# Layer 0's unit order and one set of adjacency transposes for layers 1 and 2 in a four-layer graph network

## The chip, the cores and the metric

The kernel runs on one core of one Trainium2 chip. The time is device microseconds of one execution; the profile shows one execution with the busy time of each engine: TensorE (PE, with its weight loads as PEld), VectorE (DVE), ScalarE (ACT), GpSimd (POOL) and SyncE (SP, which only issues transfers). Before the change the kernel takes 2264.58 us, the median of three runs between 2263.07 and 2265.11.

## What is computed

128 graphs of 64 nodes with 256 features pass through four layers; after each, the layer's input is added and each node's row is normalised (mean and variance over its 256 features).

- Layer 0 works on the first 25 nodes. For each of five fixed groups of them it applies two graph convolutions (256 to 512 to 256 features) with the group's adjacency plus identity, scaled on both sides by 1/sqrt(degree), and adds the results with softmax weights. The other 39 nodes only pass the norm.
- Layer 1 is one such convolution over all 64 nodes: `out = D (A + I) D x W + b`, D the diagonal of 1/sqrt(degree).
- Layer 2 is a polynomial in the row-normalised adjacency P = A / rowsum: `out = (w0 + w1 P + w2 P^2 + w3 P^3) h W + b`, with a leaky ReLU.
- Layer 3 is five steps of a gated recurrent unit (GRU): messages `h W_l` are summed along nonzero edges and drive the gates r, z and n. Each step needs the one before.

All arithmetic is fp32.

## The kernel before, in words

**Chunks.** After layer 0 the graphs go in 16 chunks of eight. A chunk is held as four pairs of graphs, so that one 128x128 block-diagonal matrix holds the adjacencies of two graphs. Two chunks at a time run through layer 3, and their steps alternate row by row, so that one chunk's gates (DVE, ACT, POOL) lie under the other's matrix products (PE).

**Order.** The instruction order on PE is written out by hand: PE runs what the program text says, in that order. On the other engines a planner orders the instructions by the order of the text and by when it thinks an operand is ready. Every engine runs its own queue strictly in order, so an instruction that waits holds up all behind it.

**Layer 0** runs over 16 units, each one group of nodes for up to four tiles of graphs (groups 1, 2, 3, 4, then 0; the last seven units are group 0). For a unit:

- `load0` brings the adjacency rows `a` and the features `xg`. For the first three units POOL issues the `xg` loads, for all others SyncE does.
- `prep` (L336) adds the identity, sums the degrees (L354), takes their power on POOL (`inv_sqrt`, L122), forms the block-diagonal A0 on DVE (L359) with the constant mask `block0`, transposes it on PE (L367) and scales it into AT on DVE (L370).
- `aggregate` (L380) multiplies the features by AT, `hidden` (L394) and `support` (L408) apply the two weight matrices, `add` (L430) aggregates again and adds into F. For group 0 `finish` (L465) transposes back, adds the input and takes the norm.

A loop over i (L525) staggers these: add(i-1), aggregate(i+1), support(i), finish(i-1), hidden(i+1), prep(i+2), and then one tile of the other 39 nodes (`load_others`, `others`, `store_others`: load xo, statistics at L133, scale at L148, store). All of these loads and stores are issued by SyncE, and all weights of the five groups are requested at the start (L502 to L506).

**Layers 1 and 2** of a chunk are the generator `mid` (L210), with a `yield` between the steps: Ab (block-diagonal adjacency), A01 (its nonzero pattern), the degree factors; A1, both factors of layer 1 applied before and after its transpose; Ab divided by the row sums; two sets of four transposes (L241 for layer 1, L247 for layer 2); the polynomial by two sets of products (L255, L261), with `gather` (L201, aggregation for layer 1) between them; the products with layer 1's weights (L270) and the norm; the second gather; the products with layer 2's weights (L286) and the norm. `layernorm` (L127) does statistics on DVE, the power on POOL (L138) and the scaling on ACT (L145) in one go.

For chunks 0 and 1 these steps are placed within the last layer-0 units (`early`, L518). For later chunks they are the `filler` of the layer-3 rows: one step at the end of every row, and one in the middle of every even row (L823).

**Layer 3.** A row s of the loop at L804 issues, for one chunk x and the chunk w of the row before, the seven products of a two-by-two block scheme for the gates r and z (`x.rz(i)`) and n (`x.n(i)`, `w.n(i)`). `Gates.product` (L663) accumulates in a PSUM bank and copies partial sums away on ACT (L671). `w.n(3)` and `w.n(4)` end in the update of h; `w.turn` transposes it (L695), `w.close` gathers the next messages.

PSUM is two pools: five banks (`pg`) and three (`pt`). Layer 0 takes from both in turn, the steps of `mid` and the transposes of layer 3 from the three.

Of the kernel before, what the change touches and what calls it, by code (L numbers as in the profile page):

```python
# [1 line left out]

# [1 line left out]

# [5 lines left out]
F32 = mybir.dt.float32  # L10
AF = mybir.ActivationFunctionType
# [56 lines left out]
def gnn_stack(  # L68
# [55 lines left out]
        nc.vector.scalar_tensor_tensor(o, v, 0.0, r, op0=ALU.not_equal, op1=ALU.mult)  # L124
        return o

    def layernorm(y, by="v", n=NP, r=128):  # L127

        by = (by * n)[:n]
        st = small.tile([128, NP, 6], F32, name="st")  # L130
        mv = small.tile([128, NP, 2], F32, name="mv")
        for p in range(n):
            nc.vector.bn_stats(st[:r, p, :], y[:r, p, :])  # L133
            nc.vector.bn_aggr(mv[:r, p, :], st[:r, p, :])
        ve = small.tile([128, NP], F32, name="ve")
        nc.vector.tensor_scalar(ve[:r, :n], mv[:r, :n, 1], EPS_LN, None, op0=ALU.add)  # L136
        rs = small.tile([128, NP], F32, name="rs")
        nc.gpsimd.tensor_tensor(rs[:r, :n], ve[:r, :n], mhalf[:r, :n], ALU.pow)  # L138
        if "a" in by:
            nb = small.tile([128, NP], F32, name="nb")  # L140
            nc.vector.scalar_tensor_tensor(nb[:r, :n], mv[:r, :n, 0], -1.0, rs[:r, :n], op0=ALU.mult, op1=ALU.mult)  # L141
        for p in range(n):
            v = y[:r, p, :]
            if by[p] == "a":
                nc.scalar.activation(v, v, AF.Identity, bias=nb[:r, p : p + 1], scale=rs[:r, p : p + 1])  # L145
            else:
                e = nc.vector if by[p] == "v" else nc.gpsimd
                e.tensor_scalar(v, v, mv[:r, p, 0:1], rs[:r, p : p + 1], op0=ALU.subtract, op1=ALU.mult)  # L148

    def interleave(*gens):  # L150
        gens = list(gens)
# [58 lines left out]
    def mid(c):  # L210

        a64 = adjs.pop(c)


        Ab = keep.tile([128, NP, 128], F32, name="Ab", bufs=1)
        nc.vector.tensor_mul(
            Ab.rearrange("p q (b m) -> p q b m", b=2),
            a64[:, :, None, :].to_broadcast([128, NP, 2, N]),
            pair[:, None, :, :].to_broadcast([128, NP, 2, N]),
        )  # L220
        A01 = keep.tile([128, NP, 128], F32, name="A01", bufs=4)
        nc.vector.tensor_scalar(A01, Ab, 0.0, None, op0=ALU.not_equal)
        rsum = small.tile([128, NP], F32, name="rsum")
        nc.vector.tensor_reduce(rsum, a64, AX.X, ALU.add)
        rdeg = small.tile([128, NP], F32, name="rdeg")
        nc.vector.tensor_scalar(rdeg, rsum, 1.0, None, op0=ALU.add)
        rinv = small.tile([128, NP], F32, name="rinv")
        nc.vector.tensor_scalar(rinv, rsum, 1e-9, None, op0=ALU.add)
        nc.vector.reciprocal(rinv, rinv)
        dinv1 = inv_sqrt(rdeg, NP, 128, "d1")  # L230
        A1 = keep.tile([128, NP, 128], F32, name="A1", bufs=1)
        nc.vector.tensor_add(A1, Ab, ident[:, None, :].to_broadcast([128, NP, 128]))
        nc.vector.tensor_mul(A1, A1, dinv1[:, :, None].to_broadcast([128, NP, 128]))
        nc.vector.tensor_mul(Ab, Ab, rinv[:, :, None].to_broadcast([128, NP, 128]))
        yield


        AT1 = keep.tile([128, NP, 128], F32, name="AT1", bufs=1)
        p = psum("pT1").rearrange("p (q n) -> p q n", q=NP)
        for q in range(NP):  # L240
            nc.tensor.transpose(p[:, q, :], A1[:, q, :], ident)  # L241
        nc.vector.tensor_mul(AT1, p, dinv1[:, :, None].to_broadcast([128, NP, 128]))

        poly = keep.tile([128, NP, 128], F32, tag="poly", name="poly3", bufs=2)
        p = psum("pT2").rearrange("p (q n) -> p q n", q=NP)
        for q in range(NP):
            nc.tensor.transpose(p[:, q, :], Ab[:, q, :], ident)  # L247
        nc.vector.scalar_tensor_tensor(
            poly, p, cw[:, 3:4], cI[:, 2, None, :].to_broadcast([128, NP, 128]), op0=ALU.mult, op1=ALU.add
        )  # L250
        yield
        xt = xts.pop(c)
        p = psum("pp").rearrange("p (q n) -> p q n", q=NP)
        for q in range(NP):
            nc.tensor.matmul(p[:, q, :], Ab[:, q, :], poly[:, q, :], start=True, stop=True)  # L255
        poly = keep.tile([128, NP, 128], F32, tag="poly", name="poly1", bufs=2)
        nc.vector.tensor_add(poly, p, cI[:, 1, None, :].to_broadcast([128, NP, 128]))
        ag = gather(xt, AT1, "ag1")
        p = psum("pp").rearrange("p (q n) -> p q n", q=NP)
        for q in range(NP):  # L260
            nc.tensor.matmul(p[:, q, :], Ab[:, q, :], poly[:, q, :], start=True, stop=True)  # L261
        poly = keep.tile([128, NP, 128], F32, tag="poly", name="poly0", bufs=2)
        nc.vector.tensor_add(poly, p, cI[:, 0, None, :].to_broadcast([128, NP, 128]))
        yield
        for u in range(NP // 2):
            p = psum("pd").rearrange("p (q d) -> p q d", q=2)
            for h in range(2):
                q = 2 * u + h
                for k in range(2):
                    nc.tensor.matmul(  # L270
                        p[:, h, :], ag[:, k, q * 128 : (q + 1) * 128], L1W[:, k, :], start=k == 0, stop=k == 1
                    )
            nc.vector.tensor_add(xt[:, 2 * u : 2 * u + 2, :], p, xt[:, 2 * u : 2 * u + 2, :])
        nc.vector.tensor_add(xt, xt, l1bs[:, None, :].to_broadcast([128, NP, D]))
        layernorm(xt, "a")
        yield


        ag = gather(xt, poly, "ag2")
        yield  # L280
        for u in range(NP // 2):
            p = psum("pd").rearrange("p (q d) -> p q d", q=2)
            for h in range(2):
                q = 2 * u + h
                for k in range(2):
                    nc.tensor.matmul(  # L286
                        p[:, h, :], ag[:, k, q * 128 : (q + 1) * 128], L2W[:, k, :], start=k == 0, stop=k == 1
                    )
            v = keep.tile([128, 2, D], F32, name="v", bufs=1)
            nc.scalar.activation(v, p, AF.Identity, bias=cb)  # L290
            nc.vector.scalar_tensor_tensor(v, v, 0.2, v, op0=ALU.mult, op1=ALU.max)
            nc.vector.tensor_add(xt[:, 2 * u : 2 * u + 2, :], v, xt[:, 2 * u : 2 * u + 2, :])
        layernorm(xt, "a")
        state[c] = (xt, A01)
        yield

# [11 lines left out]
    with ExitStack() as c0:  # L308
# [6 lines left out]

        loads, A, AG, HG, S2, Z, XO = {}, {}, {}, {}, {}, {}, {}

        def load0(i):
            u = UNITS[i]

            qa = [nc.scalar, nc.sync] if i == 0 else [nc.sync]
# [3 lines left out]
            for t, (b0, nb) in enumerate(u.tiles):  # L325
                b = slice(b0, b0 + nb)
                row = 0
                for f, m in RUNS[u.g]:
# [1 line left out]
                    row += nb * m  # L330
                    w = u.n if u.g < 2 else NE
                    qa[t % len(qa)].dma_start(a[rows, t, :w], adj[b, f : f + m, 0:w])
                    qx.dma_start(xg[rows, t, :], x[b, f : f + m, :])
            loads[i] = a, xg

        def prep(i):  # L336
# [162 lines left out]
        b1 = const(b1T, [128, NG * 4], "b1", nc.scalar, w0)  # L499
        b2c = const(b2.rearrange("g (k p) -> p (g k)", p=128), [128, NG * 2], "b2", nc.scalar, w0)  # L500
        fw = spread(fusion_w, NG, "fw", w0, nc.scalar)
        for g in (1, 2, 3, 4, 0):  # L502
            nc.sync.dma_start(W1[:, g], w1[g].rearrange("(k p) e -> p k e", p=128))
            nc.sync.dma_start(W2[:, g], w2[g].rearrange("(k p) e -> p k e", p=128))
            if g in (1, 2):
                load0(g)  # L506

        def products(l, q):

# [7 lines left out]

        early = both(mid(0), mid(1))  # L518

        def stage(f, i, first=0):  # L520
            if first <= i < NU:
                f(i)

        g0 = next(i for i, u in enumerate(UNITS) if u.g == 0)
        for i in range(-2, NU + 1):  # L525
# [1 line left out]
                stage(load0, i + 3)  # L527
            stage(add, i - 1)
            stage(aggregate, i + 1)
            if i > g0 + 2:  # L530
                next(early, None)
            stage(support, i)
            if i == NU:
                folds = [products(0, q) for q in range(3)]
            stage(finish, i - 1, g0)
            if i > g0:
                next(early, None)
            stage(hidden, i + 1)
            if i > g0:
                next(early, None)  # L540
            stage(prep, i + 2)
            for f, o in ((store_others, i - 1), (others, i), (load_others, i + 2)):
                if 0 <= o < 10:
                    f(o)
# [15 lines left out]
            elif i == 1:  # L560
# [9 lines left out]
                    mask = const_later(maskT, [128, B // 2], "mask")  # L570
                brz = wp.tile([128, 4], F32, name="brz")
                nc.vector.tensor_add(brz, bih[:, 0:4], bhh[:, 0:4])


                cI = wp.tile([128, 3, 128], F32, name="cI")
                for k in range(3):
                    nc.vector.tensor_scalar(cI[:, k, :], ident, cw[:, k : k + 1], None, op0=ALU.mult)
            elif i == 4:

                ih = keep.tile([128, 4, 2, D], F32, tag="RZ", name="ih", bufs=2)  # L580
# [59 lines left out]
    class Gates:  # L640
# [22 lines left out]
        def product(self, i):  # L663
# [3 lines left out]
            if i in (1, 6, 7, 4):  # L667
                self.multiply(self.a, i)
                if i != 4:
                    c = self.copies[i] = work.tile([128, 2, H], F32, tag="copy", name=f"c{i}", bufs=4)  # L670
                    nc.scalar.copy(c, self.a)  # L671
                if i == 7:
                    nc.vector.tensor_add(C[:, :, 1, H:], self.d, self.copies.pop(7))  # L673
            elif i == 2:
# [129 lines left out]
    for s in range(NCH * L):  # L804
# [15 lines left out]
        if w:  # L820
            w.n(3)
        x.rz(6)
        if t % 2 == 0:  # L823
            next(filler, None)
        x.rz(5)
        x.rz(7)
        x.n(1)
# [91 lines left out]
```

## Time and profile before

| | us |
|---|---|
| time, median of 3 | 2264.58 |
| span of the profiled execution | 2265.5 |
| PE busy / idle in it | 2198.4 / 67.1 |
| DVE, ACT, POOL busy | 1328.4, 1047.5, 587.5 |
| PE busy in 0 to 123 us (layer 0, first seven units) | 92.9 |
| PE busy in 123 to 223 us (layer 0, next units) | 100.0 |
| PE busy in 223 to 385 us (layer 0's end, chunks 0 and 1, weights of layer 3) | 148.9 |
| PE busy in 411 to 600 us, 600 to 838 us (layer 3) | 188.4 of 189, 236.6 of 238 |
| PE busy in 2220 to 2265.5 us (tail) | 29.8 |

A line of the profile names the source line, the engine, the operation, the output and the inputs, the shapes and a count, then the busy time and the mean of one, and last the idle time of the engine just before, with what ended it. In a list of single instructions the first number is the start in us and the second the length. A matrix product in fp32 appears as two records (L241 and the other transposes as one). In the list of waits each line says which engine at which line waited for which, how long in total, how often, and the longest.

### The profile page before, as it was taken

The page shows a single profiled execution, that of the slowest core. Times are in us where ns is not written, and L with a number is a line of the kernel's source. Part 1 is how long each engine was busy: PE and PEld are TensorE (multiplying, and loading weights), DVE is VectorE, ACT ScalarE, POOL GpSimd, SP SyncE. Part 2 cuts the span into 40 slices and gives each one's busy share as a digit, 9 for nine tenths or more (in the row PEclk, how much of TensorE's full clock was granted, in tenths as well). Part 3 has the DMA queues.
Part 4 walks back from the last instruction along what each step waited for, and adds up shares of the span by engine and source line. Part 5 has one row for each costly group of instructions (what it writes and reads, how often), then busy time and mean ns, then how long its engine had stood idle before and what let it go on. Part 6 is the DMA issues. An engine that isn't in the chain of part 4 may idle for free.

```text
span 2265.5 us, 30226 instructions
## 1 busy us (share of the span) xinstructions
PE 2198.4 (97%) x11590; PEld 1920.0 (85%) x11590; DVE 1328.4 (59%) x2927; ACT 1047.5 (46%) x1930; POOL 587.5 (26%) x639
## 2 busy tenths in 40 slices
PE   5999999999999999999999999999999999999997
PEld 4777778888888888888888888988889888888886
DVE  4433446655765656556666575566665665556546
ACT  2333334454545454544544544445454545455453
POOL 3210104222232222322322222222222222223222
PEclk9999999999999999999999999999999999999998
DMA  7530200000000001000100010000000000000000
GB/s 203 167 104 12 64 21 28 3 1 3 19 22 1 3 10 31 1 3 1 38 3 3 1 38 3 3 1 24 17 1 1 19 10 1 1 6 15 1 1 19
DMA packets 53892, 51.12 MB, mean 23 GB/s; under 512 B 20598, under 2 KB 48630, under 8 KB 53748
## 3 DMA queue, kind: packets, MB, share of 16 engines
q1 hardware_dynamic: 49524, 43.90, 6.4%
q0 software_dynamic: 1936, 4.83, 0.8%
q8 instruction: 91, 1.49, 0.3%
q10 hardware_dynamic: 2288, 0.47, 0.1%
q14 instruction: 53, 0.43, 0.1%
HBM read 32.40 MB, written 16.78 MB: 22 GB/s over the span
## 4 chain that ended last, share of the span: by engine, by line
PE 77%; DVE 12%; DMA 4%; ACT 2%; issue 2%; POOL 1%; SPq 1%; POOLq 0%; DVEq 0%; ACTq 0%
PE parz L655 21%; PE pan L655 10%; PE pdrz L655 10%; PE pa L201 8%; PE pdn L655 5%; PE pbrz L655 5%; PE ps L408 3%; PE pT L695 3%; PE pbn L655 3%; PE pd L286 2%; PE ph L394 2%; DVE st L133 2%; DMA xo<-in_x_dram 1%; ACT xt L145 1%; POOL rs L138 1%
## 5 line engine op out<-in xcount | busy, mean ns | idle before, releaser
L671 ACT COPY c<-parz 128x512 f32<-128x512 f32 x240 | 140.2, 584 | 362.6 <-PE parz L655 362.6
L655 PE MATMUL parz<-Th,WHH 128*128 128x256 f32 x960 | 285.9, 379 | 0.0
L655 PE MATMUL parz<-Ta,V 128*128 128x256 f32 x960 | 285.5, 379 | 0.0
L635 POOL TENSOR_TENSOR Th<-hn 128x512 f32<-128x512 f32 x64 | 93.4, 1460 | 630.2 <-DVE hn L755 630.2
L752 ACT ACTIVATE NI<-NI,bih 128x512 f32<-128x512 f32 x160 | 115.5, 722 | 228.2 <-DVE NI L748 228.2
L655 PEld LDWEIGHTS parz<-Ta,V 128*128 128x128 f32 x960 | 182.4, 190 | 24.8
L635 POOL TENSOR_TENSOR Ta<-agg 128x512 f32<-128x512 f32 x80 | 101.5, 1269 | 363.9 <-ACT agg L204 363.9
L655 PEld LDWEIGHTS parz<-Th,WHH 128*128 128x128 f32 x960 | 176.1, 190 | 21.1 <-ACT c L671 0.5
L683 DVE TENSOR_TENSOR RZ<-pdrz,c 128x512 f32<-128x512 f32 x80 | 55.1, 689 | 223.5 <-PE pdrz L655 223.4
L671 ACT COPY c<-pan 128x512 f32<-128x512 f32 x240 | 140.4, 585 | 94.6 <-PE pan L655 94.6
L725 ACT ACTIVATE RZ<-RZ,brz 128x512 f32<-128x512 f32 x160 | 106.8, 716 | 121.4 <-DVE RZ L683 121.4
L655 PE MATMUL pan<-Ta,V 128*128 128x256 f32 x480 | 143.2, 380 | 0.9 <-ACT c L671 0.9
L655 PE MATMUL pan<-Th,WHH 128*128 128x256 f32 x480 | 142.8, 379 | 0.0
L138 POOL TENSOR_TENSOR rs<-ve,mhalf 128x4 f32<-128x4 f32 (+2 forms) x66 | 66.3, 1004 | 264.4 <-DVE ve L136 264.1
L677 DVE TENSOR_TENSOR NI<-pbn,c 128x512 f32<-128x512 f32 x80 | 55.3, 691 | 132.9 <-PE pbn L655 130.1
L201 PEld LDWEIGHTS pa<-A,h 128*128 128x128 f32 x1024 | 123.5, 192 | 10.4 <-ACT h L769 7.6
L201 PE MATMUL pa<-A,h 128*128 128x128 f32 x1024 | 125.8, 276 | 3.2 <-ACT h L769 3.2
L673 DVE TENSOR_TENSOR NI<-pdn,c 128x512 f32<-128x512 f32 x80 | 54.7, 684 | 102.4 <-ACT c L671 102.4
L145 ACT ACTIVATE xt<-xt,nb,rs 128x256 f32<-128x256 f32 x186 | 98.0, 590 | 33.0 <-DVE nb L141 32.7
L754 DVE TENSOR_TENSOR RZ<-RZ 128x512 f32<-128x512 f32 x160 | 109.8, 686 | 2.4
L755 DVE TENSOR_TENSOR hn<-RZ,NI 128x512 f32<-128x512 f32 x160 | 109.8, 686 | 2.2
L753 DVE TENSOR_TENSOR RZ<-hn,NI 128x512 f32<-128x512 f32 x128 | 87.9, 687 | 36.6 <-ACT NI L752 36.3
(200 smaller groups left out, 5090.9 us busy)
## 6 DMA issues: line engine op xcount, KB each, us to landing
out_dram<-xt SPq DMA_DIRECT2D x32, 256.0 KB
W<-in_w_dram SPq DMA_DIRECT2D x10, 512.0 KB
xt<-xb SPq DMA_DIRECT2D x32, 156.0 KB
xo<-in_x_dram SPq DMA_DIRECT2D x9, 512.0 KB
xb<-xo SPq DMA_DIRECT2D x9, 512.0 KB
xt<-xa SPq DMA_DIRECT2D x32, 100.0 KB
xg<-in_x_dram SPq DMA_DIRECT2D x25, 125.0 KB
xa<-xg SPq DMA_DIRECT2D x25, 125.0 KB
```

The costliest lines, as they stand in the source:

```text
L138: nc.gpsimd.tensor_tensor(rs[:r, :n], ve[:r, :n], mhalf[:r, :n], ALU.pow)
L145: nc.scalar.activation(v, v, AF.Identity, bias=nb[:r, p : p + 1], scale=rs[:r, p : p + 1])
L201: nc.tensor.matmul(p[:, q * 128 : (q + 1) * 128], src[:, q, k * 128 : (k + 1) * 128], m[:, q, :], start=True, stop=True)
L408: nc.tensor.matmul(p[: u.rows[t], t - v, :], hg[:, e, u.off[t] : u.off[t] + u.rows[t]], W2[:, u.g, e, :], start=e == 0, stop=e == 3,)
L635: nc.gpsimd.tensor_sub(t[:, 0:2, :], a[:, :, H:], a[:, 0, :].rearrange("p (s n) -> p s n", s=2))
L655: nc.tensor.matmul(bank[:, g, :], w[:, q, i - 1, :], rhs, start=i in (1, 2, 5) and g == 0 and m == 0, stop=m == len(side) - 1, skip_group_ ...
L671: nc.scalar.copy(c, self.a)
L725: nc.scalar.activation(RZ[:, q, 0, :], RZ[:, q, 0, :], AF.Sigmoid, bias=b[0])
L752: nc.scalar.activation(n, n, AF.Tanh, bias=bih[:, 4 + j : 5 + j])
L753: nc.vector.tensor_sub(d, self.hT[:, j, :], n)
L754: nc.vector.tensor_mul(d, d, z)
L755: nc.vector.tensor_add(self.hn[:, j, :], d, n)
```

## The change

It has four parts.

1. One set of transposes. Layer 1 needs the transpose of A + I, layer 2 that of P. Both now come from one transpose of Ab itself: for layer 1 the identity and the inner degree factor are applied to the result on DVE, the outer factor where the product with layer 1's weights is added to x. For layer 2 the polynomial is carried on diag(rowsum) times itself (`dg` in place of `cI`), and the missing 1/rowsum is applied by ACT when the product with layer 2's weights is read. The bias of layer 1 is added to x earlier.
2. The norm of `mid` in two steps, `norm_stats` and `norm_apply`, with a `yield` between them. The steps get places of their own in the last layer-0 units (`places`), and the filler runs in the middle of every row of layer 3.
3. Layer 0: prep(i+2) stands before hidden(i+1), the `xg` loads of units 1 and 2 wait for the power of the unit before, prep(1) is planned after the eviction of unit 0's transposes, and the weights of a group are requested when it is near.
4. The copies of the gate sums have a higher priority for the planner.

```
+        dg = keep.tile([128, NP, 128], F32, name="dg", bufs=1)
+        nc.vector.tensor_mul(dg, ident..., rsum...)
+        nc.vector.tensor_mul(An, Ab, rinv...)
...
-            nc.tensor.transpose(p[:, q, :], A1[:, q, :], ident)
-        nc.vector.tensor_mul(AT1, p, dinv1[:, :, None].to_broadcast([128, NP, 128]))
...
             nc.tensor.transpose(p[:, q, :], Ab[:, q, :], ident)
-        nc.vector.scalar_tensor_tensor(poly, p, cw[:, 3:4], cI[:, 2, ...], op0=ALU.mult, op1=ALU.add)
+        nc.scalar.activation(poly, p, AF.Identity, scale=cw[:, 3:4])
+        nc.vector.scalar_tensor_tensor(poly, dg, cw[:, 2:3], poly, op0=ALU.mult, op1=ALU.add)
+        nc.vector.tensor_add(AT1, p, ident...)
+        nc.vector.tensor_mul(AT1, AT1, dinv1...)
...
-        nc.vector.tensor_add(poly, p, cI[:, 1, None, :].to_broadcast([128, NP, 128]))
+        nc.vector.scalar_tensor_tensor(poly, dg, cw[:, 1:2], p, op0=ALU.mult, op1=ALU.add)
         ag = gather(xt, AT1, "ag1")
+        nc.vector.tensor_add(xt, xt, l1bs[:, None, :].to_broadcast([128, NP, D]))
...
-            nc.vector.tensor_add(xt[:, 2 * u : 2 * u + 2, :], p, xt[:, 2 * u : 2 * u + 2, :])
-        nc.vector.tensor_add(xt, xt, l1bs[:, None, :].to_broadcast([128, NP, D]))
-        layernorm(xt, "a")
+            for h in range(2):
+                nc.vector.scalar_tensor_tensor(xt[:, q, :], p[:, h, :], dinv1[:, q : q + 1], xt[:, q, :], ...)
+        norm = norm_stats(xt, "a")
+        yield
+        norm_apply(xt, *norm, "a")
...
-            nc.scalar.activation(v, p, AF.Identity, bias=cb)
+            for h in range(2):
+                nc.scalar.activation(v[:, h, :], p[:, h, :], AF.Identity, bias=cb, scale=rinv[:, q : q + 1])
...
-        for g in (1, 2, 3, 4, 0):
-            ... both weights of g; if g in (1, 2): load0(g)
+        load_weights(1)
...
+        places = [(1, 1), (1, 2), (2, 1), (2, 2), (2, 2), (3, 1), (3, 2), (3, 2)]
+        places += [(4, 0), (4, 0), (4, 1), (4, 2), (4, 2), (5, 1), (5, 2), (5, 2)]
...
             stage(aggregate, i + 1)
-            if i > g0 + 2:
-                next(early, None)
+            early_stage(i, 0)
             stage(support, i)
...
+            early_stage(i, 1)
+            if i == -1:
+                with tc.issue_after(evictions[0].ins):
+                    prep(1)
+            else:
+                stage(prep, i + 2)
+            if i < 0:
+                load0(i + 3, powers[-1])
+                load_weights(i + 4)
             stage(hidden, i + 1)
-            if i > g0:
-                next(early, None)
-            stage(prep, i + 2)
+            early_stage(i, 2)
+            if i == 0:
+                for g in (4, 0):
+                    load_weights(g)
...
-                    nc.scalar.copy(c, self.a)
+                    with tc.high_priority():
+                        nc.scalar.copy(c, self.a)
...
-        if t % 2 == 0:
-            next(filler, None)
+        next(filler, None)
```

## The prediction

> **What bounds the kernel now.** I read the page first, then the chain, then who waited for whom on TensorE, then single stretches in order of time.
>
> ```profile
> PE 2198.4 (97%) x11590; PEld 1920.0 (85%) x11590; DVE 1328.4 (59%) x2927; ACT 1047.5 (46%) x1930; POOL 587.5 (26%) x639
> ...
> PEclk9999999999999999999999999999999999999998
> ...
> PE 77%; DVE 12%; DMA 4%; ACT 2%; issue 2%; POOL 1%; SPq 1%; POOLq 0%; DVEq 0%; ACTq 0%
> ```
>
> TensorE (PE) is busy 97% of the span and is 77% of the chain. So a change can save in three ways only: fewer PE instructions, less of the 67 us in which PE is idle (2265.5 - 2198.4), and less time at a reduced PE clock. The waits of PE over the whole span (total us, times, longest us) say where the idle time lies:
>
> ```profile
> PE pT L367 <- DVE A L359: 19.3, 1, 19.3
> PE pa L380 <- DVE AT L370: 11.2, 6, 4.6
> PE pa L201 <- ACT xt L145: 7.1, 2, 3.6
> PE pT L695 <- DVE hn L755: 5.7, 2, 4.1
> PE pT L247 <- ACT agg L204: 5.0, 6, 0.8
> PE pa L201 <- ACT h L769: 3.2, 11, 0.4
> ```
>
> By stage: 0 to 123 us (layer 0's first seven units) has 30.1 us idle, 123 to 223 none, 223 to 385 13.1, the recurrent part from 411 to 2030 8.2, the tail after 2220 15.7. The first wait, on VectorE (DVE) at the start:
>
> ```profile
> 5.97 0.16 DVE L120 TENSOR_TENSOR d0s<-deg,d0z 126x4 f32<-126x4 f32 x1
> 16.27 0.20 DVE L348 TENSOR_TENSOR ae<-a,eye 126x36 f32<-126x36 f32 x1 [10.14 <-DMA a<-in_adj_dram]
> ...
> 17.01 0.15 DVE L124 SCALAR_TENSOR_TENSOR d0o<-deg,d0r 126x4 f32<-126x4 f32 x1
> ...
> 18.52 0.68 DVE L359 TENSOR_TENSOR A<-ae,block 126x504 f32<-126x504 f32 x1
> ```
>
> Unit 0's degrees are there at 6.1, and GpSimd (POOL) has their power at 8.8. But unit 1's first operation stands ahead on DVE and waits for its adjacency until 16.27; only then does unit 0 go on. And this is what a wait costs PE beyond itself (start, length):
>
> ```profile
> 235.71 1.95 PE L201 MATMUL pa<-AT,xt 128*128 128x128 f32 x16
> ...
> 258.00 3.71 PE L201 MATMUL pa<-poly,xt 128*128 128x128 f32 x16 [3.47 <-ACT xt L145]
> ```
>
> The same sixteen records take 1.95 us, and 3.71 after a wait of 3.47.
>
> **What the Trainium skill says.** "TensorE: Matmul & The Clock Gate", section "What's actually happening": the PE clock halves after an idle window of about 3.4 us and comes back after about as long a busy one. The trace agrees on the doubling (3.71 against 1.95), but here even 1.89 us of idle time is followed by it (3.36 at 81.85 against 1.96 for the same shape). "DMA: Bandwidth & Descriptors", section "Issuing engines are not separate DMA queues": loads started by different engines interleave on the same 16 DMA engines. The trace agrees: between 6 and 14 us their mean busy share is 1.06 to 1.12, while three engines issue. "Perfetto Trace Analysis", section "Optimization Strategy": look for the gaps of the most contended engine and for what ends them. That is the method above.
>
> **The change, part by part.** What stands ahead of what on an engine is read for the changed kernel from the order of its built instructions.
>
> *One set of transposes.* Each of the 16 chunks loses four 128x128 transposes (L241: x64, 9.6 us of records). Four of them move what follows by 0.44 us (222.15 to 222.59), 0.109 us each. 64 x 0.109 = **7.0 us** off PE, sure, as PE is the bound. DVE stays level: two passes over A1 go and dg and the add of the identity come (0.69 us each, starts 0.60 apart); two adds of pd (0.68) become four half-width ones (0.48). ACT gains one eviction (0.69) and two halves (about 0.49 each for one of 0.69), about 1.3 us a chunk, 21 us in all on an engine that is 46% busy: nothing on the path.
>
> *Norms in two steps.* In the stage of 223 to 385 us the gather of layer 2 stood behind one aggregate only, and waited for the norm: 258.00, 8.6 us after the products (L270) it depends on had ended at 249.4, and again at 316.07. Now it comes after add, aggregate, support and finish of the next unit: 1.8 + 1.8 + 7.0 + 0.9 = 11.5 us of PE work (10.5 for the short last unit). That hides 8.6. So 7.1 us of waits go, and the slow stretches after them: (3.71-1.95) + (7.92-7.07) + (3.98-1.95) + (7.76-7.07) = 5.3. The wait of 1.1 of the second transpose for a bank goes too. The second chunk's preparation and transposes are now called together, but its only input for them was on chip long before. I take **12.5** of 13.5; the low end, if the half-width evictions hold a bank longer, is 9.
>
> *Recurrent part.* The second transposes waited 0.8 us six times for a bank that ACT had not emptied; there are none now: 5.0. The gather of A01 waited 3.2 in all for a copy of h queued on ACT behind the norm's four activations (0.59 each); the norm is now applied elsewhere, and the copies of the gate sums have priority. Against it: the polynomial products and the first gather now stand in the middle of an odd row, right behind w.n(3). There pp is followed by a gather of 1.79 us and by the second pp, which needs poly1. DVE then has the work of w.n(3) in front: in the row at 424 us the last of it in front of poly1 (L748) ends 3.4 us after the end of PE's pdn; poly1 adds 0.75. PE needs 1.73 + 0.89 + 1.79 = 4.4 us to the second pp. So about 0.25 us of slack: wait 0 at the low end, about 1 us a chunk at the high end (14 chunks, 14 us). I take 2 in all: 8.2 - 2 = **6**; range +8 to -6.
>
> *The start.* Unit 0 no longer stands behind unit 1 on DVE, nor its power behind two other units' ten xg loads on POOL (1.34 to 7.60). What is left is the block mask: the load queue stood 0.7 us for it until 11.72. So A is done near 11.7 + 0.7, and PE's transposes start at about 12, not 19.25. AT follows directly: about 1 us of wait, not 3.1. But unit 1's transposes now come before unit 0's hidden products on PE (**the added wait**; all of PE is behind it). On DVE, unit 1's factors stand behind the first statistics of xo, whose load is issued near 14.3 after two weights: 1.57 MB at the 330 GB/s of 16.5 to 30.8 us, so about 19.7. A of unit 1 is ready near 21.5; PE waits some 5 us and starts hidden slowly (+2) at about 22, where it was 27.0; the second aggregate starts at 30, not 35.5. From there the queue of loads (about 0.75 us an issue, never empty from 21 to 123 us) runs some 4 us earlier, since the weights of the last two groups go behind unit 3. And each AT now has its transposes one hidden (7 us) earlier: the evictions behind xo loads (0.5, 1.9 and 4.6 us of PE waits at 66, 82 and 123; the last AT stood behind the tenth xo, now behind the eighth) should come in time: with 4 us gained, AT of unit 6 is ready at 105.5 and wanted at 109.7, of unit 7 at 122.3 and 124. Idle: 30.1 becomes 12 + 1 + 5 + 0.5 = 18.5, so 11.6 less; slow stretches lost at 82 (1.4 + 0.4) and 123 (1.8 + 2.0), 5.6, less the new 2: **15.2**. Bounds: 7, if loads come no sooner and PE runs into them two units later; 19, if xo lands 4 us sooner.
>
> *At nothing:* l1bs added earlier and cI gone (DVE is 59% busy); the tail is untouched.
>
> Sum: 7.0 + 12.5 + 6 + 15.2 = 40.7; 2264.6 - 40.7 = **2224**.
>
> **The rivals.**
>
> A. *The load queue keeps the pace at the start.* For it: the chain from 21 to 115 us runs almost only through issues at SyncE and xo loads. Against it: in the worst stretch the wait was for an eviction queued wrongly, not for its own data. Start 5 instead of 15: 2234.
>
> B. *The second pp waits in each chunk.* DVE was busy without a gap from 419 to 437 us in such a row, so a queue of 1.5 us is possible: 14 x 1.5 = 21, 2245. Against it: the 4.4 us just counted.
>
> C. *Slower.* The steps now fill rows 0 to 7 of ten with two each. If DVE's backlog pushes hn past its transposes in the 56 rows by 0.9 us, 50 us come on top: 2274. Against it: L695 waited for hn only in the tail; hn of side 0 has 8 us between w.n(3) and its transpose.
>
> **How the numbers follow.** Forecast 0.60, A 0.20, B 0.13, C 0.05, the rest (2%) a greater gain. Ends of the sum: 7 + 9 - 6 + 7 = 17 and 7 + 13.5 + 8 + 19 = 47.5; all low ends together are unlikely. Range 2214 to 2243. Faster by over 0.2% (below 2260): 0.93; same 0.02; slower 0.05.
>
> **What would show it.** PE's records fewer by 64, its busy time less by about 16 (7.0 of work, 8.9 of slow clock), its idle time by about 25. First transposes near 12 us; a wait of L389 of some 5 us near 21, and waits of L402 for AT below 1 us each. No wait of L209 for the norm in the layer-0 stage. Recurrent rows without the 0.8 us waits; waits of L272 for poly1 under 0.3 us each. It is wrong if L272 or L729 waits in most chunks, or if L402 waits for AT behind an xo as before.

## The result, and the profile after

The changed kernel takes 2249.28 us (median of 6 runs, 2242.6 to 2251.51), the kernel before 2264.85: ratio 0.9927, 95% interval 0.9912 to 0.9942. The forecast was 2224, with 2214 to 2243 as its range. So the change is faster, as forecast, but by 15.6 us and not by 40.7; the time is outside the range. Most of the missing gain was lost in one stage, as three sums by stage from the two traces show (us; the forecast has its transposes put where they are removed):

| stage | before | forecast of the change | after | change found |
|---|---|---|---|---|
| to the first finish (pse) of a unit of group 0 | 214.57 | -15.2 | 202.27 | -12.3 |
| from there to the first gate product | 162.89 | -12.5 - 0.9 | 150.43 | -12.5 |
| recurrent part and tail | 1888.04 | -6.1 - 6.0 | 1895.80 | **+7.8** |

The last stage is most of the error: 12.1 less was said, 7.8 more was found, 19.9 us apart of the 23.7 between forecast and these two executions. The same stages of the changed kernel, by engine (window, its length, then busy us and instructions of PE, PEld, DVE, ACT, POOL):

```profile
0.00:202.27 202.27, 182.58 (x860) 135.17 (x861) 84.75 (x354) 65.51 (x111) 46.67 (x62) 0.98 0.44 133
202.27:352.70 150.43, 144.27 (x772) 118.25 (x770) 91.37 (x267) 62.49 (x135) 35.68 (x47) 0.99 0.15 46
352.70:2248.50 1895.80, 1860.92 (x9897) 1656.29 (x9895) 1193.02 (x2352) 936.17 (x1732) 521.04 (x531) 1.00 0.03 9
```

In the last line PE is busy 1860.9 of 1895.8 us, 34.9 idle; before it was 1864.1 of 1888.0, 23.9 idle. So 56 transposes went and 11 us of waiting came. In the whole span PE has 64 records less, as forecast (11526 for 11590), but its busy time fell by 10.6 us to 2187.8, where about 16 was said, and its idle time by 6.4 to 60.7, where about 25 was said. Over the whole span, the waits of TensorE in the changed kernel (total us, times, longest):

```profile
PE pT L389 <- DVE A L381: 13.0, 1, 13.0
PE pa L209 <- ACT h L803: 9.6, 14, 0.7
PE pp L272 <- DVE poly L267: 7.2, 7, 1.3
PE pT L729 <- DVE hn L789: 5.4, 2, 4.1
PE pT L389 <- DVE fs L591: 3.4, 1, 3.4
PE pa L402 <- DVE AT L392: 3.3, 2, 2.5
PE po L452 <- ACT s L439: 3.0, 1, 3.0
PE pp L272 <- DVE d1z L118: 2.7, 5, 0.5
```

The first line was 19.3, the one of L402 was 11.2, and the 7.1 us for the norm and the 5.0 for a bank are gone, as forecast but for one wait of 2.5 of L402. Three lines are new or grown: **the copy of h** (3.2 before, now 9.6, once a chunk), **the second pp product** (L272: 9.9 in 12 waits, in both its lines), and one wait of 3.0 for a copy of s at 315 us.

*The copy of h.* ScalarE (ACT), VectorE (DVE) and PE in the first of these rows (start, length), and ACT in such a row of the kernel before:

```profile
439.54 0.60 ACT L150 ACTIVATE xt<-xt,nb,rs 128x256 f32<-128x256 f32 x1 [1.46 <-DVE nb L142]
440.04 0.45 ACT L757 ACTIVATE RZ<-parz,brz 128x256 f32<-128x256 f32 x1
440.40 0.57 ACT L803 COPY h<-pT 128x512 f32<-128x512 f32 x1
```
```profile
439.34 0.16 DVE L142 SCALAR_TENSOR_TENSOR nb<-mv,rs 128x4 f32<-128x4 f32 x1 [1.12 <-POOL rs L138]
```
```profile
441.02 1.16 PE L209 MATMUL pa<-A,h 128*128 128x128 f32 x8 [0.69 <-ACT h L803]
```
```profile
437.84 1.09 ACT L145 ACTIVATE xt<-xt,nb,rs 128x256 f32<-128x256 f32 x2 [0.70 <-DVE nb L141]
438.83 0.56 ACT L769 COPY h<-pT 128x512 f32<-128x512 f32 x1
```

ACT sits idle for 1.46 us with the application of the second layer's norm at the head of its queue, waiting for nb, which waits for GpSimd's power. The copy of h stands behind it; PE's gather waits until 441.02. In the row before, ACT was idle for 0.70 and two activations stood ahead of the copy; the gather waited 0.23.

*The second pp product.* PE and DVE where it waits longest:

```profile
613.11 0.59 PE L688 MATMUL parz<-Th,WHH 128*128 128x256 f32 x2
...
618.97 1.13 PE L272 MATMUL pp<-poly,An 128*128 128x128 f32 x8 [1.29 <-DVE poly L267]
```
```profile
613.82 0.68 DVE L711 TENSOR_TENSOR RZ<-pbrz,c 128x512 f32<-128x512 f32 x1
...
615.01 0.68 DVE L787 TENSOR_TENSOR RZ<-hT,NI 128x512 f32<-128x512 f32 x1
615.61 0.74 DVE L781 SCALAR_TENSOR_TENSOR NI<-NI,bhh,RZ 128x512 f32<-128x512 f32 x1
616.28 0.68 DVE L788 TENSOR_TENSOR RZ<-RZ 128x512 f32<-128x512 f32 x1
616.88 0.68 DVE L782 TENSOR_TENSOR NI<-NI 128x512 f32<-128x512 f32 x1
617.48 0.68 DVE L789 TENSOR_TENSOR hn<-RZ,NI 128x512 f32<-128x512 f32 x1
618.08 0.73 DVE L267 SCALAR_TENSOR_TENSOR poly<-dg,cw,pp 128x512 f32<-128x512 f32 x1
```

PE is through with pdn at 613.11, where its next product starts. DVE comes to the add of pbrz (L711) only 0.71 us after that. Then the three passes of an update of hn (L787 to L789) and two others stand in front of poly1, each 0.6 to 0.7 us from start to start. In the row of the kernel before that the prediction counted, DVE came to the same add 0.32 us *before* PE was through with pdn:

```profile
424.37 0.59 PE L655 MATMUL parz<-Th,WHH 128*128 128x256 f32 x2
```
```profile
424.05 0.68 DVE L677 TENSOR_TENSOR RZ<-pbrz,c 128x512 f32<-128x512 f32 x1
```

The chunks are not alike. In five the second pp waits 1.29 us, and DVE comes to the add 0.71 after pdn, as here; in five it waits 0.54, and DVE comes 0.05 before; one waits 0.3, one 0.5, two do not wait.

### The profile page after: what moved, and what is told of

It reads as the page before. It is cut to its first block, busy times and chain, and to the rows that moved or that the text cites. A ratio compares the mean times of both kernels' runs of the same rounds, so it can differ in the third digit from the quotient of the medians.

```text
span 2248.5 us, 30146 instructions
## 1 busy us (share of the span) xinstructions
PE 2187.8 (97%) x11526; PEld 1909.7 (85%) x11526; DVE 1369.1 (61%) x2972; ACT 1064.2 (47%) x1978; POOL 603.4 (27%) x639
## 4 chain that ended last, share of the span: by engine, by line
PE 75%; DVE 13%; ACT 3%; DMA 3%; SPq 2%; issue 2%; POOL 1%; ACTq 0%; POOLq 0%; DVEq 0%
PE parz L688 20%; PE pan L688 10%; PE pdrz L688 10%; PE pa L209 7%; PE pdn L688 5%; PE pbrz L688 5%; PE pT L729 3%; PE ps L430 3%; PE pbn L688 3%; PE pd L281 2%; PE ph L416 2%; DVE st L133 1%; PE pd L302 1%; DMA xo<-in_x_dram 1%; DVE v L309 1%
## 5 line engine op out<-in xcount | busy, mean ns | idle before, releaser
L668 POOL TENSOR_TENSOR Th<-hn 128x512 f32<-128x512 f32 x64 | 89.3, 1395 | 651.5 <-DVE hn L789 642.1
L668 POOL TENSOR_TENSOR Ta<-agg 128x512 f32<-128x512 f32 x80 | 101.6, 1270 | 377.9 <-ACT agg L212 377.9
L711 DVE TENSOR_TENSOR NI<-pbn,c 128x512 f32<-128x512 f32 x80 | 55.3, 691 | 137.5 <-PE pbn L688 135.1
L209 PEld LDWEIGHTS pa<-A,h 128*128 128x128 f32 x1024 | 123.2, 192 | 17.8 <-ACT h L803 15.2
L209 PE MATMUL pa<-A,h 128*128 128x128 f32 x1024 | 126.1, 276 | 9.6 <-ACT h L803 9.6
L787 DVE TENSOR_TENSOR RZ<-hn,NI 128x512 f32<-128x512 f32 x128 | 87.9, 687 | 53.0 <-ACT NI L786 53.0
L789 DVE TENSOR_TENSOR hn<-RZ,NI 128x512 f32<-128x512 f32 x160 | 109.6, 685 | 1.8
```

Of the source, the lines that this page charges most:

```text
L209: nc.tensor.matmul(p[:, q * 128 : (q + 1) * 128], src[:, q, k * 128 : (k + 1) * 128], m[:, q, :], start=True, stop=True)
L668: nc.gpsimd.tensor_sub(t[:, 0:2, :], a[:, :, H:], a[:, 0, :].rearrange("p (s n) -> p s n", s=2))
L787: nc.vector.tensor_sub(d, self.hT[:, j, :], n)
L789: nc.vector.tensor_add(self.hn[:, j, :], d, n)
```

## The experiments

For e1 to e3, e5 and e9 to e11, the two places of the row loop that call the filler (after x.rz(6), and after x.n(5)) got a written plan, one pair (row, 0 for the middle or 1 for the end) for each of a chunk's eight steps; the second chunk of a pair has the same, four rows on. The first line is what the changed kernel does; e9 to e11 have the plan of e2:

```diff
-    plan = [(0,0), (0,1), (1,0), (1,1), (2,0), (2,1), (3,0), (3,1)]
+    plan = [(0,0), (0,1), (1,1), (2,0), (2,0), (2,1), (3,0), (3,1)]   e1
+    plan = [(0,0), (0,1), (1,0), (1,1), (2,0), (2,1), (3,1), (4,0)]   e2
+    plan = [(0,0), (0,1), (1,1), (2,0), (2,0), (2,1), (3,1), (4,0)]   e3
+    plan = [(0,0), (0,1), (1,1), (2,0), (2,1), (3,0), (3,1), (4,0)]   e5
```

All results; each ratio is to runs of the kernel before taken beside them (medians 2264.85 to 2266.77), with the recurrent part and tail of the profiled execution (from the first gate product to the end):

| kernel | median us | ratio to before, 95% interval | recurrent part and tail |
|---|---|---|---|
| before | 2264.85 | 1 | 1888.0 |
| changed | 2249.28 | 0.9912 to 0.9942 | 1895.8 |
| e1_pp_late | 2247.61 | 0.9907 to 0.9932 | 1895.3 |
| e2_norm2_late | 2237.62 | 0.9862 to 0.9889 | 1885.8 |
| e3_both_late | 2236.68 | 0.986 to 0.9887 | 1885.0 |
| e4_layer0_order | 2255.35 | 0.9939 to 0.9966 | 1887.8 |
| e5_apply_later | 2240.26 | 0.9868 to 0.9895 | 1887.1 |
| e6_one_set | 2342.09 | 1.0316 to 1.0344 | 1970.2 |
| e7_no_priority | 2250.38 | 0.9912 to 0.9937 | 1896.1 |
| e8_xo_behind | 2256.55 | 0.994 to 0.9967 | 1895.9 |
| e9_pp_split | 2227.64 | 0.9813 to 0.9839 | 1877.5 |
| e10_best | 2221.56 | 0.979 to 0.9815 | 1877.4 |
| e11_two_sets | 2248.78 | 0.9912 to 0.9937 | 1892.9 |
| e12_one_set_priority | 2255.6 | 0.9939 to 0.9962 | 1884.8 |

**The second norm's place (e2).**

> The changed kernel with one move: the seventh step (pd2 and the second layer's statistics) from the middle of row 3 to its end, where the kernel before had it, and the eighth (its application) from the end of row 3 to the middle of row 4. Theory (the application, waiting on ScalarE for nb, holds up the h copy): the L209 waits on the h copy of L803 fall from 14 with 9.6 us to at most 4 with 3 us, the L272 waits stay at about 10 us; time 2249.3 - 6.5 = 2243. Rival (fuller engines): time within 2 us of 2249; the wait comes back in row 4, on another copy.

Measured: 2237.6, 11.7 less than the changed kernel, and in the recurrent part 10.0 less (1895.8 to 1885.8), for 9.6 us of waits. In its waits, L209 behind L803 is gone, and L272 is as it was:

```profile
PE pp L272 <- DVE poly L267: 7.3, 7, 1.3
...
PE pp L272 <- DVE d1z L118: 2.7, 5, 0.5
```

So half of what this stage lost is this one place: statistics in the middle of a row and application at its end put the application ahead of the row's copies of h.

**The third step's place (e1, e3, e5).**

> The changed kernel with one move in the recurrent rows: of the eight steps of a chunk's filler, the third (the pp products with poly1, and the first gather) goes back from the middle of row 1 to its end, the transposes staying at the end of row 0, and statistics and application of the first norm both go to the middle of row 2. Theory (the nearness of poly1's chain to its product makes the wait): the waits of L272 on DVE, 12 of them with 9.9 us in the changed kernel, fall under 3 us, the h-copy waits of L209 (9.6 us) stay; time 2249.3 - 7 = 2242, and no worse than 2245. Rival (vector and scalar engines are simply fuller, the waits only move to another instruction): PE idle in the recurrent stretch stays at 18 to 20 us and the time within 2 us of 2249.

> The changed kernel with both moves (third step at the end of row 1, seventh at the end of row 3, eighth in the middle of row 4). Theory: both waits go, PE idle in the recurrent stretch falls from 19.6 to 5 to 7 us, time 2249.3 - 13.5 = 2236. Rival (the added 40 us of VectorE work and the stretched instructions are the cause wherever they stand): at most 5 us gained, time 2244 to 2250.

Measured: e1 gained 1.7, e3 0.9 over e2, neither clear of the scatter of the runs: nearly what the rival said of e1, although the L272 waits for poly1 did go. The time went into another wait (pan behind a gate copy, 4.8 us in 15, where it was 0.9 in 1) and into late starts too short to be listed: PE is busy 1865.9 us in e1's recurrent part and 1860.9 in the changed kernel's, with the same 9897 instructions (a product's record ends some 0.16 us after the start of the next one, 0.59 long and 0.43 from start to start, so a short late start shows as busy time). In e3, ACT shows why:

```profile
642.41 0.59 ACT L705 COPY c<-parz 128x512 f32<-128x512 f32 x1 [4.37 <-PE parz L688]
644.92 0.60 ACT L150 ACTIVATE xt<-xt,nb,rs 128x256 f32<-128x256 f32 x1 [1.92 <-DVE nb L142]
645.43 0.57 ACT L705 COPY c<-pan 128x512 f32<-128x512 f32 x1
645.89 0.59 ACT L803 COPY h<-pT 128x512 f32<-128x512 f32 x1
```

It is the picture of the h copy again, at the *first* norm: moving the third step moved the fourth (pd1 and the statistics) into the middle of row 2, where nb comes late and two copies stand behind the application. So e1 and e3 changed two things and could not tell whether DVE has room for poly1. e5 was to part them:

> The changed kernel with the filler's third step at the end of row 1 as in e3, but the fifth (application of the first norm) half a row after the fourth, at the end of row 2, the sixth (second gather) in the middle of row 3, the seventh at the end of row 3, the eighth in the middle of row 4. Theory: what e3 left, 3.9 us of waits of the pan products for a gate copy and as much again in small late starts near them, comes from the application standing in ScalarE's queue between a gate product and its copy; with the application elsewhere the recurrent stretch and tail, 1885.0 us in e3, fall to about 1879, time 2236.7 - 6 = 2231. Rival (ScalarE and VectorE have no room anywhere): 2235 to 2240, with a wait of the same size at another line.

Measured: no gain (2240.3; 1887.1), the pan waits the same 4.7 us. The row order binds only PE; ACT's planner put the application in front of the copy all the same (644.16 ahead of 644.67, as above). Moving a step's call need not move its instructions on the other engines.

**The second pp alone (e9).** On top of e2:

```diff
         ag = gather(xt, AT1, "ag1")
         nc.vector.tensor_add(xt, xt, l1bs[:, None, :].to_broadcast([128, NP, D]))
+        yield
         p = psum("pp").rearrange("p (q n) -> p q n", q=NP)
...
         nc.vector.scalar_tensor_tensor(poly, dg, cw[:, 0:1], p, op0=ALU.mult, op1=ALU.add)
-        yield
```

> e2 (second layer's statistics at the end of row 3, application in the middle of row 4) with one more edit: the second pp product and its eviction (poly0) go from the third filler step to the head of the fourth, half a row later, so that poly1 has that half row to be made; everything else keeps its place, the statistics of the first norm too. Theory (L272's waits for poly1 are the rest of what the recurrent part lost; in e1 and e3 they were bought off with another wait because the statistics moved too): no waits of L272 for poly1, no new pan waits, recurrent stretch and tail 1885.8 - 10 = 1876, time 2237.6 - 10 = 2228. Rival (the vector engine has no room, as e1 and e3 seem to say): 2235 to 2238, with the time back at another line.

Measured: 2227.6. In the recurrent part 8.2 less than e2, 18.3 less than the changed kernel, and 10.5 less than before, where the prediction had said 12.1. The two pp products (the second is now L273; count, busy us, mean ns, idle before) wait for nothing:

```profile
L265 PE MATMUL pp<-poly,An 128*128 128x128 f32 x128 | 16.9, 275 | 0.0
L273 PE MATMUL pp<-poly,An 128*128 128x128 f32 x128 | 16.9, 275 | 0.0
```

And the recurrent part and tail, to be held against the third window of the changed kernel above:

```profile
349.87:2227.40 1877.53, 1859.55 (x9897) 1652.82 (x9895) 1165.47 (x2352) 936.45 (x1732) 507.05 (x531) 1.00 0.03 9
```

poly1 itself is made no sooner: in the chunk shown above it ends 5.72 us after pdn, where it was 5.71. Only the product that needs it now stands half a row later. What is left of the 12.1 is 1.6, beside a new small wait of pdrz for an add of DVE, 1.7 us in five.

**Is it the transposes, or the load on VectorE? (e6, e12, e11)**

> The kernel before with the first part of the change alone: one set of transposes and the degree factors on results, norms in one step, filler steps and layer 0 as before, no raised priority. Theory (the first part is harmless by itself; the recurrent part was lost by where steps were put): 7.0 us of transposes and 5.0 us of bank waits go, nothing comes, 2264.9 - 12 = 2253, recurrent stretch and tail 1888.0 - 11 = 1877. Rival (40 us more of VectorE work, and instructions stretched beside GpSimd, is what cost the recurrent part): 2258 to 2266.

> e6 (the kernel before with the first part alone, 76 us slower than before) with the raised priority of the gate copies. Theory (in e6 the gate copies stand behind the norm's four activations, which wait for GpSimd's power; the priority puts them ahead): the pan and parz waits for copies, 68 us in e6, fall under 10, time 2342 - 76 - 12 = 2254, and under 2275 in any case. Rival (only taking the application apart from the statistics does it; the copy is not ready when the planner places the application): over 2320.

e6 was 76 us slower than before, which neither theory had. Its worst waits, and ACT ahead of one:

```profile
PE pan L658 <- ACT c L674: 49.6, 15, 3.5
...
PE parz L658 <- ACT c L674: 18.9, 14, 1.4
```
```profile
531.34 1.09 ACT L145 ACTIVATE xt<-xt,nb,rs 128x256 f32<-128x256 f32 x2 [1.92 <-DVE nb L141]
532.33 0.56 ACT L772 COPY h<-pT 128x512 f32<-128x512 f32 x1
532.80 1.09 ACT L145 ACTIVATE xt<-xt,nb,rs 128x256 f32<-128x256 f32 x2
...
535.05 0.58 ACT L674 COPY c<-pan 128x512 f32<-128x512 f32 x1
```

Four activations of the norm, the first of them idle for nb, and a copy of h stand ahead of the copy that PE needs. With the priority on the copies alone (e12) the pan line falls to 4.3 us and the parz line to 0.2, and the time to 2255.6, 1.6 from what was expected. DVE is busy 1156.3 us in the recurrent part, where before it was 1153.5: the first part of the change puts 2.8 us on it, not 40. What can cost far more is the order on ACT that comes with it. The 11.2 us gained do not lie where I expected them, though: 3.3 in the recurrent part (1884.8), and 7.7 in the stage before it (155.2 for 162.9). In the recurrent part the pan waits cost 3.4 more than before, and PE is busy 1.3 us longer although 56 transposes are gone: late starts as in e1. In the stage before it the wait for the norm fell from 7.1 us to 1.8 with the norms still in one step. The bias, added earlier, no longer stands between the products and the statistics (1.22 us on DVE at L274 before); whether that is the reason, no run shows.

> e2 with the first part of the change undone: two sets of transposes with the degree factors on the operands, as before; norms in two steps, filler places as e2, layer 0 and priorities as changed. Theory (the poly1 waits come from the new chain, ScalarE eviction and one more VectorE pass ahead of the first pp product): the L272 waits of 10 us are gone, 7.0 us of transposes are back, bank waits of up to 5 us back: recurrent stretch and tail 1885.8 - 10 + 6.1 + 0 to 5 = 1882 to 1887, time 2234 to 2239. Rival (the place of the third step makes those waits, whichever way the factors are put on): the L272 waits stay and the time is 2244 to 2249.

The time, 2248.8, is the rival's, but not its mechanism. L269, its second pp, waits for poly1 nowhere, and the bank waits are back. Against e2 the recurrent part is 7.1 longer (1892.9), 6 more than the upper end of my sum, of which 2.2 are waits of parz for a copy, 0.2 in each of 14; the rest of the time was lost in layer 0, in waits that are no part of this question (4.3 for a load of x, 4.6 of po; the profiled execution is the slowest of the six).

```profile
PE pT L255 <- ACT agg L212: 5.0, 6, 0.8
```
```profile
622.14 0.69 DVE L706 TENSOR_TENSOR RZ<-pbrz,c 128x512 f32<-128x512 f32 x1 [0.85 <-ACT NI L781]
```
```profile
622.73 0.59 PE L683 MATMUL parz<-Th,WHH 128*128 128x256 f32 x2
```

The last two lines are of the chunk that waited 1.29 us in the changed kernel. The passes between the add of pbrz and poly1 are the same, the three of an update among them, but DVE comes to that add 0.59 us before the end of pdn (0.61 in one chunk), in all 14 chunks. So the poly1 waits come from the new, longer chain together with the product's place: the old chain has two passes of DVE between the transposes and the first pp product (L250, L256), the new one three (L257, L259, L260), and either the old chain (e11) or half a row more (e9) takes the waits away.

One more thing can be read from e11. It has the transposes and the chain of the kernel before, and its recurrent part is 4.9 longer (1892.9 for 1888.0): in the recurrent rows, norms in two steps at these places gain nothing by themselves.

**The priority alone (e7).** The changed kernel with one line undone:

```diff
-                    with tc.high_priority():
-                        nc.scalar.copy(c, self.a)
+                    nc.scalar.copy(c, self.a)
```

> The changed kernel without the raised priority of the gate copies. Theory (the priority is neither the cause of the new waits nor the cure): within 3 us of 2249. Rival 1 (the copies, pushed ahead, delay the gather copies and so poly1): 5 us or more faster, the L272 waits gone. Rival 2 (without it the copies stand behind the norm's activations): 4 to 12 us slower, with new waits of the pan and parz products for copies.

Measured: 2250.4, 1.1 from the changed kernel, the same waits. With norms in two steps the priority is not needed; with one set of transposes and norms in one step (e6 against e12) it is worth 86 us.

**The start (e4, e8, e10).**

> The kernel before with the third part of the change alone: weights and loads of the first units in the new order, x loads held back behind the first square root, the second unit's preparation first and every preparation ahead of the hidden products; transposes, norms and recurrent rows as before. Theory (the start's 12.3 us at the first finish are all from this part and are kept to the end): 2264.9 - 12 = 2253. Rival (the gain at the start needs the two-step norms, or comes back in the last units): 2257 to 2265.

Measured: 2255.4, a gain of 10.5 of the 12.

> The changed kernel with VectorE's statistics of each xo kept behind the last eviction of AT of the preparation in the same pass, and the last step of chunk 1 (application of its second norm) one unit later; the rest as changed. Theory (in the start the miss is an instruction standing in VectorE's queue behind an xo load, not the loads): wait of L389 near 21 from 3.4 to under 0.5, wait of L402 near 112 (2.5, and 1.7 of slow products after it) gone, wait of L452 near 315 (3.0, and 1.5 of slow products) gone: 2249.3 - 12 = 2237. Rival (the loads set the pace, so the waits only move to the next unit): 2245 or more.

The edit:

```diff
-                    f(o)
+                    with tc.issue_after(evictions[-1].ins) if f is others else nullcontext():
+                        f(o)
```

Measured: 2256.6, slower by 7. No wait of L402 near 112, but two new things on DVE:

```profile
19.57 0.17 DVE L370 TENSOR_TENSOR ae<-a,eye 126x9 f32<-126x9 f32 x1 [2.15 <-DMA a<-in_adj_dram]
19.65 0.68 DVE L381 TENSOR_TENSOR A<-ae,block 126x504 f32<-126x504 f32 x1
...
135.60 0.69 DVE L224 TENSOR_TENSOR Ab<-a,pair 128x512 f32<-128x512 f32 x1 [18.85 <-DMA a<-in_adj_dram]
136.21 0.68 DVE L392 TENSOR_TENSOR AT<-pT,d0o 126x504 f32<-126x504 f32 x1
```

With the xo statistics away, unit 1's A stands behind unit 2's first add, which waits for its load (the wait of L389 is 3.1, not under 0.5). And the planner now put the first pass of chunk 0 in front of an eviction of AT; its load came at 135.6, and PE waited 13.6 us. Half of the rival was right, then: the wait moved to the next instruction that waits for a load. e10 is e9 with this edit, chunk 0's first step kept behind the evictions too, and chunk 1's last step one unit later:

> e9 with the statistics of each xo kept behind the last eviction of AT of the same pass as in e8, and, so that the first step of chunk 0 does not run ahead of the evictions as it did there, that step kept behind them too; the last step of chunk 1 one unit later. Theory: the wait of 2.5 us near 112 and 1.7 of slow products after it go, of the 3.0 near 315 half stays: e9 - 6 = 2222. Rival (the loads set the pace, or another early instruction takes the place): no faster than e9, within 2 us.

Measured: 2221.6, 6.1 less than e9 and 27.7 less than the changed kernel; the runs of e9 and e10 do not overlap. But the wait that the theory named is not what went. In the changed kernel's profile L402 waited 2.52 at 111.89; the profiles of e9 and e10 have no wait at this product:

```profile
110.35 1.90 PE L402 MATMUL pa<-AT,xg 126*128 126x126 f32 x12
```
```profile
106.38 1.90 PE L402 MATMUL pa<-AT,xg 126*128 126x126 f32 x12
```

What these two profiles show is a start that is 4.8 us shorter (first finish at 194.65 for 199.40; the wait near 21 is 2.4 for 3.2, and the hidden products after it take 6.93 for 8.67), and a next stage that is 2.9 shorter, in which the wait near 315 fell from 2.97 to 1.48. How much of the start is the edit's, and how much is the execution that was profiled, stays open.

## Why the prediction was wrong, step by step

- *One set of transposes: 7.0 us off PE.* **Right.** PE has 64 records less, and with the two waits taken away (e9) the recurrent part is 10.5 shorter than before, 6.1 of it transposes. "DVE stays level" holds for the sum (1156.3 us in e12, 1153.5 before), but the sum leaves out the place: of five passes, three stood ahead of the transposes and two behind them, and now it is two and three. In the changed kernel the sum is 1193.0, as instructions last longer; see the end.
- *Norms in two steps: 12.5.* **Right in size, not wholly in cause.** The stage is 12.5 shorter, 0.9 of it transposes; but e12, with norms in one step, has 7.7 of these too, and e11, with the old transposes and norms in two steps, has 6.7. So the two parts share the gain, the two steps alone are worth less than was said, and that the size came out is in part luck. The bias added earlier, which was put at nothing, may have a share in it. The two waits for the norm are gone; a wait of 3.0 for the copy of s, behind chunk 1's application, was not foreseen.
- *The recurrent part: 6 us less, and its share of the transposes.* **The step that failed.** Two sentences of it were wrong.
  "The gather of A01 waited 3.2 in all for a copy of h queued on ACT behind the norm's four activations (0.59 each); the norm is now applied elsewhere": it went from 3.2 to 9.6. I took the four activations' length for the cost and the program's step for the place. The cost is the idle time of the *first* activation, waiting for nb from the statistics by way of GpSimd's power, and the application lies in ACT's queue wherever the planner puts it. Moving it took the waits away and 10.0 us (e2).
  "So about 0.25 us of slack" for the second pp: this was counted in a row of the kernel before, with the old chain's queue on DVE. There DVE was 0.32 us ahead of the end of pdn; in the changed kernel it was 0.71 behind in five chunks, 1.03 later. And one pass was left out of the count: of the three of an update of hn, the third (L789, L755 before) stands ahead of poly1 too, 0.6. 1.03 + 0.60 - 0.25 is 1.38 where 1.29 was found; in the five chunks where DVE was 0.27 later the same sum gives 0.62, and 0.54 was found. In all it was 9.9 where 2 was taken. With the old chain (e11) the waits are gone, and with the product half a row later (e9) they are gone with 8.2 us. It is rival B's mechanism, a queue on DVE, in 12 chunks of 14, at 0.8 us a wait in the mean where B had 1.5; but rival B alone would have left 2245, and it had a chance of only 0.13.
  10.0 + 8.2 of the 19.9 us are thus shown; the rest is 1.6.
- *The start: 15.2.* **Right in kind, the size open by some us.** First transposes at 13.0 (said: 12), a wait of 3.4 near 21 (said: 5), second aggregate at 30.98 (said: 30). At 112 L402 waited behind an xo load again, which was said to be wrong if seen. No other profile has that wait: e1, e2, e3, e5, e7 and e9, with the same layer 0, have at most 0.39 there and reach the first finish at 197.7 to 199.4, 198.6 in the mean, against 214.4 for the three profiles with the old order (before, e6, e12): 15.8 less. The runs of e4 say 10.5 (its profile, of the fastest of its five, has the first finish at 198.1), and the medians of the changed kernel, less what the other two stages show, 10.9 (15.6 - 12.5 + 7.8). I leave it at 10 to 16. One figure of the sum was misread: between 16.5 and 30.8 us the loads moved 360 GB/s, not 330, so that the first xo would have been there at 18.7 by that count; it came at 20.33.
- *Rivals.* A (start of 5 us) is not what happened. C neither: L729 waits for hn in the tail only, 5.4 us.

## What to carry to other kernels

Where one engine is busy all the time, count for each edit what stands in the *other* engines' queues in front of the instruction that the bound engine needs, in the queue as the edit leaves it and not in a row of the old kernel, and waiting instructions first: an activation of 0.6 us that was short of its operand cost 0.7 us a chunk in the changed kernel, and up to 3.5 in e6 with more of its kind in front of the copy. Split a step so that a product and the chain that feeds it lie half a row apart. Where a planner orders an engine, the place of a call need not be the place of its instructions: read it from the trace, and move one step at a time (e1 moved two, and hid its own answer).

## What the runs showed of the hardware

The same instruction lasted up to twice as long beside GpSimd. L309 (two operands in SBUF) on DVE in the changed kernel and in e9 (count, busy us, mean ns, idle before):

```profile
L309 DVE SCALAR_TENSOR_TENSOR v<-v 128x512 f32<-128x512 f32 x32 | 31.4, 981 | 8.5 <-ACT v L308 8.5
```
```profile
L309 DVE SCALAR_TENSOR_TENSOR v<-v 128x512 f32<-128x512 f32 x32 | 22.0, 688 | 48.6 <-ACT v L308 48.6
```

The Trainium skill says so: "SBUF — State Buffer", section "SBUF: two separate sides", states that a VectorE operation with two SBUF inputs and a GpSimd operation that reads SBUF hold their shared ports in turn, each for its whole length. The trace agrees: the L309 that started at 434.02, beside GpSimd's L668 (until 434.85), lasted 1.38, and L669, beside it, 1.06, where it is 0.73 alone. It is so in the queue ahead of poly1 too (DVE, then POOL, in the chunk that waited 1.29):

```profile
610.31 0.68 DVE L259 TENSOR_TENSOR AT<-pT,ident 128x512 f32<-128x512 f32 x1
...
611.30 1.21 DVE L260 TENSOR_TENSOR AT<-AT,d1o 128x512 f32<-128x512 f32 x1
```
```profile
609.91 1.06 POOL L669 TENSOR_TENSOR Ta<-agg,Ta 128x256 f32<-128x256 f32 x1
611.05 0.91 POOL L670 TENSOR_TENSOR Ta<-agg,Ta 128x256 f32<-128x256 f32 x1
```

L260 has both operands in SBUF and lasted 1.21 (0.68 at 469.30, with no GpSimd beside it); L259, with one operand in PSUM, kept its 0.68 beside L669. L257 or L260 lasted over 1.0 us in 13 of the 16 chunks. In e11 the two passes in their place read pT from PSUM, and they took 0.69 and 0.75 in all 16. How much of the waits for poly1 is this, and how much the third pass itself, no run separates.

DVE's 2352 instructions of the recurrent part were busy 1193.0 us in the changed kernel and 1165.5 in e9, 27.5 less with the same work; L309 and L310 alone are 14.5 of that. So most of the 40 us that DVE seemed to have gained was not work. No engine waited for L309 itself.

The waits for poly1 cost no clock: the granted PE clock was 1.00 from 619.0 to 622.0, after the wait of 1.29 us. After the 2.52 at 111.89 it was 0.80 from 113.81 to 122.50.
